# Two attention blocks in fp32: the second layer's value product is divided in halves twice, its score sums and factor sums get fixed places, and the last two sub-product groups of each twice divided convolution are interleaved in a new order

## The chip, the cores and the metric

The kernel runs on one core of one Trainium2 chip. The metric is the time on the device of one execution, in microseconds. The kernel before takes 2795.72 us (median of three runs, 2795.53 to 2796.02). A separate execution was recorded by the profiler, and every duration below that isn't called a run's comes from that record.

The names of the engines are those of the profile: PE is the matrix engine (PEld is its loading of weights, which overlaps the matmuls), DVE the vector engine, ACT the scalar engine, POOL the general engine, SP the engine whose queue issues nearly all DMA transfers.

## The reference, cut to what matters

Eight images x of 512 channels and 32 x 32 = 1024 tokens go through two layers, all in fp32. Layer 0 is attention with eight heads, layer 1 attention with one:

```python
def layer0(x):                                  # x: (8, 512, 1024)
    h = group_norm(x, 32 groups)
    q, k, v = (w_qkv @ h + b_qkv) per head      # 8 heads of 64 channels
    weight = softmax(q^T k / 8)                 # per head, 1024 x 1024
    a = v weight^T
    return x + w_proj @ a + b_proj

def layer1(x):
    xn = group_norm(x, 8 groups)
    q, k, v = q_w @ xn + q_b, k_w @ xn + k_b, v_w @ xn + v_b
    attn = softmax(q^T k / sqrt(512))           # one head, 1024 x 1024
    out = attn v
    return x + p_w @ out + p_b
```

The kernel uses two products of weights in layer 1. With m made of q's and k's weights, the scores are (m h)^T h, so g = m h takes the place of q and k. With z made of v's and p's weights, the value product and the output projection are one product: z = (p_w v_w) h, and the output is x + z attn^T + bias. "Layer 1's value product" in this text is this z, 512 channels by 1024 tokens for each image.

## The kernel before, in words

**Strassen-Winograd, once and twice.** A product of two matrices is divided into quarters and made with seven products of half the size in place of eight, at the price of sums of the quarters before and after. `wino` (L229) does this once: `step(p)` runs product p, PE accumulates several products in the same PSUM bank ("a", "b" or "c", two tiles each), and ACT or DVE takes the bank out, adding what other products left (`upper`, `done`). `conv2` (L517) does it twice for a 1 x 1 convolution: each of the seven outer products is again divided, so there are 49 products. It works on the outer products in four groups, called pairs here because most hold two: `pair(0, (1, 5))`, `pair(1, (2, 6))`, `pair(2, (7,))`, `pair(3, (3, 4))`. Each pair goes to `inner_steps` (L441), which runs the seven inner products, every one for both outer products of its pair.

**The order inside a pair** is written out by hand. `inner_steps` runs product 1, which opens bank a; ACT copies the bank into bank b (L472), on which products 6, 7 and 4 then accumulate. Next comes `finish()`, which runs what the previous pair left behind, and then 6, 2, 5, 7. Products 3 and 4 are put on a list, `tail`, and so run behind product 1 of the next pair. Product 5 opens bank c, from which DVE or ACT takes `c5` before product 3 accumulates on the same bank:

```python
            step(1)
            finish()
            for g in early:
                g()
            for j in (6, 5, 2, 7) if five_first else (6, 2, 5, 7):
                step(j)
            for g in after7:
                g()
            tail.extend([lambda: step(3), lambda: step(4)])
```

The last pair of a convolution has its copy in two halves (`halved`, L471), and in the projection p its order is 6, 5, 2, 7 (`five_first`). After every step one function of the list `background` runs (`run_background(1)`), which is how sums on DVE and POOL are spread over a stage; `hooks` are functions that run after product 7 of a pair, `after7`.

**Which convolutions are divided how.** v, k, q and p of layer 0 and g (weights m) of layer 1 run in `conv2`. z runs in `by_token` (L368), once divided: 56 matmuls of 128x128 weights on 256 columns per image, with h as the stationary operand. v runs in `conv2` with `by_tokens=True`: h is stationary too, and each matmul is 128 columns wide. The product of scores with values (`values1`, L801) and the scores of layer 1 (`scores1`, L721) are divided once and twice.

**Weights.** The sums of the weights are made once, in `prologue` (L905) and during the first attention (the dictionary `later`), and stored in DRAM. `prepare` (L281) makes the first level of sums, `keep` (L296) stores it for weights that are divided once, and `keep2` (L302) makes the second level with four POOL operations and stores it in seven transfers. `load_weight` (L329) brings a weight back into a pool of three buffers in the order of the list `uses`; a twice divided weight comes in two parts.

**What an image passes through.** In the main loop (L1141) one period holds layer 0's attention of image b, then layer 1 of image b-1 and the convolutions of image b+1: attention0, g (`layer1_scores`, L1106), scores1, z, values1 (`layer1_rest`, L1117), v (`values`), k and q (`keys_and_queries`), p (`projection2`), and the attention again. The sums of h (`image_factors`, L352, the first level; `inner_factors`, L412, the second) are made ahead, those of the next image during z and values1 (`factors_ahead`, L996). One special case at the end: the last image but one has g, scores1, z and values1 behind a once divided p, and the last image has them at the very end. So z runs eight times, v in `conv2` seven times, k, q and p seven times, g eight times.

**Around z.** `scores1` ends with seven divided products whose results ACT turns into exponentials, eight tiles e[c, cc, r] of 128 x 2 x 512 (r the half of keys, c the half of queries). `add_up` (L752) sums them on POOL into two tiles `parts` and from there into `total`; two ones-matmuls' worth of column sums (`reciprocals`, L604) then give r, the reciprocals, which DVE computes from a copy that went through DRAM and came back, and which come back a last time as rows. `right_sums` (L163) makes the factor sums of e that values1 needs: eight steps t1, t2, b12, t4, each for two halves. Here four of them run on DVE and four on POOL (`engines`, L793), all from the background list. `left_sums` (L149) makes eight sums of z. In values1 `done` (L822) multiplies each output by r, adds the bias and x, and stores it.

**What sets the order on the engines.** Every matmul is wrapped in `tc.keep_in_program_order`, so PE runs them as written. On the other engines an instruction that is wrapped keeps the written order ("pinned" in this text); the others are placed by the framework's own planning. SP's queue is in the order in which transfers were issued.

Of the kernel before, what the change touches and what calls it, by code (L numbers as in the profile page):

```python
# [9 lines left out]
F32 = mybir.dt.float32  # L10
# [19 lines left out]
def two_attention_blocks_kernel(  # L30
# [143 lines left out]
    def main_path(ctx):  # L174
# [125 lines left out]
        wdram2 = {n: dram.tile([P, 7, 7, P], F32, name=f"sums2_{n}") for n in "qkmvp"}  # L300

        def keep2(n, t, engine=nc.gpsimd):  # L302

            if engine is nc.gpsimd:
                u = wpool.tile([P, 4, 7, P], F32, tag="w", name=f"prepare2_{n}")
                u = [u[:, i, :, :] for i in range(4)]
            else:
                u = [big_tile(f"prepare2_{n}_{i}", (P, 7, P)) for i in range(4)]
            quarter = lambda k, i: t[:, :, k, ts(i, P)]
            a11, a21, a12, a22 = quarter(0, 0), quarter(0, 1), quarter(1, 0), quarter(1, 1)  # L310
            s1, s2, s3, s4 = u
            for dst, x, y, op in (
                (s1, a21, a22, ALU.add), (s2, s1, a11, ALU.subtract), (s3, a11, a21, ALU.subtract),
                (s4, a12, s2, ALU.subtract),
            ):
                tc.keep_in_program_order(engine.tensor_tensor(dst, x, y, op))
            for j, f in enumerate((a11, a12, s4, a22, s1, s2, s3)):
                nc.sync.dma_start(wdram2[n][:, :, j, :], f)
# [4 lines left out]
        for b in range(1, B - 1):  # L323
            uses += [*twice["m"], "z", *layer0, *twice["p"]]
        uses += ["p", *twice["m"], "z"]
        uses += [*twice["m"], "z"]
# [114 lines left out]
        def inner_steps(uid, parity, k, mm, add, y, x, extra, after7, final, early=(), defer=None, flush=None, five_first=False, halved=False):  # L441
# [23 lines left out]
            def step(j):  # L465
                if j == 1:
                    bank("a")
                    mm(ps["a"], 1, True)

                    bank("b")  # L470
                    for part in [slice(i, i + 1) for i in range(k)] if halved else [slice(0, k)]:  # L471
                        nc.scalar.copy(ps["b"][:, part, :], ps["a"][:, part, :])  # L472
                elif j == 6:
                    mm(ps["b"], 6, False)
                    put([keep_tmp("u2", "u")], "b", (0, 1))
                    while flush:
                        flush.pop(0)()
                    extra(0, 1, True, False)
                elif j == 2:
                    mm(ps["a"], 2, False)  # L480
                    put(y(0, 0), "a", (0, 0))
                    extra(0, 0, True, True)
                elif j == 5:
                    bank("c")
                    mm(ps["c"], 5, True)
                    put([keep_tmp("c5", "w")], "c", (1, 1))
                    extra(1, 1, True, False)
                elif j == 7:
                    mm(ps["b"], 7, False)
                    add(y(1, 1), ps["b"], [tmp["c5"]])  # L490
                    extra(1, 1, False, True)
                elif j == 3:
                    mm(ps["c"], 3, False)
                    add(y(0, 1), ps["c"], [tmp["u2"]])
                    extra(0, 1, False, True)
                elif j == 4:
                    mm(ps["b"], 4, False)
                    if defer is None:
                        put(y(1, 0), "b", (1, 0))
                    else:  # L500
                        add(y(1, 0), ps["b"], x(1, 0), (0,))
                        defer.append(lambda: add(y(1, 0), ps["b"], x(1, 0), (1,)))
                    extra(1, 0, True, True)
                run_background(1)

            step(1)
            finish()
            for g in early:
                g()
            for j in (6, 5, 2, 7) if five_first else (6, 2, 5, 7):  # L510
                step(j)
            for g in after7:
                g()
            tail.extend([lambda: step(3), lambda: step(4)])
            tail.extend(final)

        def conv2(n, f, bias, name, hooks=(), after=(), by_tokens=False, alone=False):  # L517
# [43 lines left out]
            def pair(s, products, y, x, final):  # L561
# [20 lines left out]
                def extra(r, cc, read, done):  # L582
# [6 lines left out]
                inner_steps(  # L589
                    f"{name}_{s}", s % 2, len(products), mm, add, written, x and (lambda *at: blocks(x, *at)),  # L590
                    extra, hooks.pop(0) if hooks else (), final, (), second if s == 1 else None, second if s == 2 else None, five_first=alone and s == 3, halved=s == 3,
# [4 lines left out]
            pair(0, (1, 5), [(1, 0), (1, 1)], None, [])  # L596
            pair(1, (2, 6), [(0, 0), (0, 1)], [(1, 0), (1, 0)], [load_weight, lambda: biased_half(0, 0)])
            weights2.append(weight_part((n, 1)))
            pair(2, (7,), [(1, 0)], [(0, 1)], [lambda: biased_half(1, 1)])
            pair(3, (3, 4), [(0, 1), (1, 0)], [(0, 1), (1, 0)], [load_weight, *after])  # L600
# [120 lines left out]
        def scores1(f, gf, gsteps, first, uid, stats):  # L721
# [8 lines left out]
            parts = [pair_tile(f"sum{r}_{uid}") for r in range(2)]  # L730
# [21 lines left out]
            def add_up(r, c):  # L752

                on = lambda dst, x, y: lambda: tc.keep_in_program_order(nc.gpsimd.tensor_tensor(dst, x, y, ALU.add))  # L754
                if r == c:
                    return [on(parts[r], e[c, 0, r], e[c, 1, r])]
                return [
                    *(on(parts[r], parts[r], e[c, cc, r]) for cc in range(2)),
                    on(total[:, r, :], parts[r][:, 0, :], parts[r][:, 1, :]),
                ]  # L760

            def product(s, p, y, x, before, small, after7=(), final=()):
# [13 lines left out]
                inner_steps(  # L776
                    f"{uid}_{s}", s % 2, 2, mm, add, lambda *at: blocks(y, *at), x and (lambda *at: blocks(x, *at)),
                    extra, after7, final, [lambda: background.extend(small), *(lambda q=q: factors(q) for q in before)],
                )

# [7 lines left out]
                6, 4, (1, 0), (1, 0), [], stats[10:] + add_up(1, 1) + add_up(0, 1), (),  # L788
                [lambda: exps(1, 0), lambda: background.extend(add_up(1, 0) + steps)],
            )  # L790

            t = [[pair_tile(f"t{n}_{uid}_{cc}") for cc in range(2)] for n in (1, 2, 4)]
            engines = [nc.vector] * 4 + [nc.gpsimd] * 4  # L793
            fs, steps = right_sums(
                [(e[0, cc, 0], e[0, cc, 1]) for cc in range(2)], [(e[1, cc, 0], e[1, cc, 1]) for cc in range(2)],
                [lambda cc, n=n: t[n][cc] for n in range(3)],
                lambda *a: engines.pop(0).tensor_tensor(*a, ALU.subtract),
            )
            return total, {p: [x[:, i, :] for x in fs[p] for i in range(2)] for p in fs}

        def values1(b, zf, ef, r, xt, uid, hooks):  # L801
            last = b == B - 1

            def mm(p, i, ps, start):
                cut = 2 if last and (p, i) == (3, 1) else 1
                for part in range(cut):
                    cols = ts(part, HT // cut)
                    for k in range(4):
                        matmul(
                            ps[:, cols], zf[p][k // 2][:, k % 2, ts(i, P)], ef[p][k][:, cols],  # L810
                            start=start and k == 0, stop=k == 3, skip_group_check=True,
                        )

            def added(xh, o, oc):
                nc.vector.scalar_tensor_tensor(xh, o, obias[1][:, oc : oc + 1], xh, ALU.add, ALU.add)  # L815
# [6 lines left out]
            def done(i, row, c, ps, u):  # L822
# [15 lines left out]
                nc.vector.tensor_mul(o, o, r[:, c, :])  # L838
                added(xh, o, oc)
# [65 lines left out]
        def prologue():  # L905
# [46 lines left out]
            for f in p0_steps:  # L952
# [7 lines left out]
            load = lambda: load_weight(tc.keep_in_program_order)  # L960
            later = {
                3: steps, 4: [lambda: tc.keep_in_program_order(keep("z", t)), load], 8: [load], 12: [
                    load,
# [31 lines left out]

        def factors_ahead(h, loads, applies, uid):  # L996
# [3 lines left out]
            def begin():  # L1000
                for f in loads:
                    f()
                hf, t = image_factors(h, uid)
# [3 lines left out]
                hooks[3] += [*applies[2:], inner[1], *t[2:4]]  # L1007
                hooks[4] += [*inner[2:4], lambda: background.extend([*t[4:6], *inner[4:6], *t[6:], inner[6]])]
# [108 lines left out]
        def layer1_rest(b, inner, gf, gsteps, stats, hooks, ahead):  # L1117
            first = query_factors(gf[1], f"1_1_{b}")
            total, ef = scores1(inner, gf, gsteps, first, f"1_{b}", stats)
            state = {}  # L1120

            def sums():
                state["r"] = reciprocals([total], f"1_{b}", True, nc.sync)

            z = by_token(
                weight("z"), hf, f"z1_{b}", hooks=[*hooks, [sums]], back=3,
                after=[load_weight, lambda: background.extend(zsteps)],
# [3 lines left out]
            stiles = [big_tile(f"sz{i}_{b}", (P, 2, 2, C // 2)) for i in (1, 2, 4)]  # L1131
            halves = lambda t: (t[:, :, : C // 2], t[:, :, C // 2 :])
            zf, zsteps = left_sums(
                [halves(t) for t in z[:2]], [halves(t) for t in z[2:]],
                [lambda j, t=t: t[:, j, :, :] for t in stiles], nc.vector.tensor_add, nc.vector.tensor_sub,
# [3 lines left out]
        here = lambda *t: tc.keep_in_program_order(nc.vector.tensor_sub(*t))  # L1139
        x1, plan = None, {}  # L1140
        for b in range(B):  # L1141
# [31 lines left out]
            if last:  # L1173
# [12 lines left out]
                layer1_rest(b - 1, inner, gf, gsteps, stats, [[], mean, [], affine], ahead)  # L1186
# [250 lines left out]
```

## Time and profile before

| what | us |
|---|---|
| median of three runs | 2795.72 |
| profiled execution, whole | 2796.04 |
| its span, first to last instruction | 2794.2 |
| one period, attention of image 2 to attention of image 3 (first score matmuls at 664.56 and 1005.96) | 341.4 |
| in it: attention0, to the start of g at 780.35 | 115.8 |
| g, to the start of scores1 at 801.34 | 21.0 |
| scores1, to the start of z at 843.93 | 42.6 |
| z, to the start of values1 at 863.58 (two of its seven products run behind values1's first, until 877.46) | 19.7 |
| values1, to the start of v at 904.93 | 41.4 |
| v, to the start of k at 938.99 (values1's last products run between) | 34.1 |
| k, to the start of q at 960.89 | 21.9 |
| q, to the start of p at 982.28 | 21.4 |
| p, to the attention at 1005.89 | 23.6 |

How to read it: the stages overlap at their borders, since the last products of a stage run behind the first one of the next. The times are starts of matmuls. An instruction in the profile is named by its output and inputs, with buffer numbers left out, then by the number of partitions and elements; "x4" behind it is a count. In this program one fp32 matmul is shown as two passes, and a start in the trace is the time from which a pass's place in the stream can be read. An engine's busy time counts what it executes; waits for other engines' results show as idle time before an instruction, in square brackets with the name of what ended the wait.

### The profile page before, as it was taken

The page shows a single profiled execution, that of the slowest core. Times are in us where ns is not written, and L with a number is a line of the kernel's source. Part 1 is how long each engine was busy: PE and PEld are TensorE (multiplying, and loading weights), DVE is VectorE, ACT ScalarE, POOL GpSimd, SP SyncE. Part 2 cuts the span into 40 slices and gives each one's busy share as a digit, 9 for nine tenths or more (in the row PEclk, how much of TensorE's full clock was granted, in tenths as well). Part 3 has the DMA queues.
Part 4 walks back from the last instruction along what each step waited for, and adds up shares of the span by engine and source line. Part 5 has one row for each costly group of instructions (what it writes and reads, how often), then busy time and mean ns, then how long its engine had stood idle before and what let it go on. Part 6 is the DMA issues. An engine that isn't in the chain of part 4 may idle for free.

```text
span 2794.2 us, 35149 instructions
## 1 busy us (share of the span) xinstructions
PE 2781.3 (100%) x12764; PEld 1753.0 (63%) x12764; DVE 1991.5 (71%) x3022; ACT 990.9 (35%) x1311; POOL 1269.1 (45%) x1300
## 2 busy tenths in 40 slices
PE   9999999999999999999999999999999999999999
PEld 6437637676376853858538584485844868348585
DVE  6577777677777677766786767776677766787665
ACT  1253463214531246312553125531254213633130
POOL 2303605745077430865308652185612846037672
PEclk9999999999999999999999999999999999999999
DMA  7835412344113441134401443114522045112301
GB/s 263 254 132 184 179 32 70 129 156 153 39 62 134 158 154 32 62 143 161 149 24 62 162 183 108 32 54 162 203 88 63 23 152 218 54 62 88 122 3 73
DMA packets 118669, 320.10 MB, mean 115 GB/s; under 512 B 19607, under 2 KB 58199, under 8 KB 107866
## 3 DMA queue, kind: packets, MB, share of 16 engines
q1 hardware_dynamic: 117902, 317.36, 32.0%
q8 instruction: 103, 1.69, 0.2%
q14 instruction: 76, 0.62, 0.1%
q10 hardware_dynamic: 588, 0.42, 0.0%
HBM read 247.13 MB, written 70.62 MB: 114 GB/s over the span
## 4 chain that ended last, share of the span: by engine, by line
PE 99%; DVE 1%; issue 0%; DMA 0%; SPq 0%
PE sc L60 16%; PE av L60 16%; PE psb_av L60 6%; PE psb L60 5%; PE psa_av L60 4%; PE psc_av L60 4%; PE psc L60 3%; PE psa L60 3%; PE psb_z L60 3%; PE psb_v L60 3%; PE psb_g L60 3%; PE psb_q L60 3%; PE psb_k L60 3%; PE psb_p L60 3%; PE psa_z L60 2%; PE psc_z L60 2%
## 5 line engine op out<-in xcount | busy, mean ns | idle before, releaser
L669 ACT ACTIVATE e<-sc 128x1024 f32<-128x1024 f32 x512 | 476.1, 1050 | 72.9 <-PE sc L60 72.9
L673 DVE TENSOR_TENSOR sum<-sum,e 128x1024 f32<-128x1024 f32 x384 | 470.6, 1225 | 35.7 <-ACT e L669 1.1
L60 PE MATMUL sc<-q,k 64*128 64x512 f32 x2048 | 456.8, 596 | 0.0
L60 PE MATMUL av<-e,v 128*64 128x512 f32 x2048 | 453.4, 595 | 0.0
L60 PEld LDWEIGHTS sc<-q,k 64*128 64x128 f32 x2048 | 190.0, 185 | 246.1 <-ACT e L669 121.5
L60 PEld LDWEIGHTS av<-e,v 128*64 128x64 f32 x2048 | 141.4, 137 | 299.0 <-issue 288.2
L423 POOL TENSOR_TENSOR inner_h<-x 128x256 f32<-128x256 f32 x16 | 14.8, 923 | 416.2 <-DVE x L1139 416.2
L671 DVE TENSOR_TENSOR sum<-e,e 128x1024 f32<-128x1024 f32 x64 | 79.1, 1236 | 106.8 <-ACT e L669 106.8
L692 ACT COPY a<-av 128x512 f32<-128x512 f32 x64 | 37.5, 587 | 320.0 <-PE av L60 280.5
L126 POOL TENSOR_TENSOR rstd<-ve,mhalf 128x4 f32<-128x4 f32 x16 | 19.4, 1210 | 265.8 <-DVE ve L124 265.8
L60 PE MATMUL psb<-inner,inner_h 128*128 128x256 f32 x448 | 115.6, 380 | 0.0
L60 PE MATMUL psa_av<-e,z 128*128 128x512 f32 x256 | 113.3, 595 | 0.0
L423 POOL TENSOR_TENSOR inner_h<-h 128x256 f32<-128x256 f32 x30 | 25.2, 841 | 180.3 <-DVE h L1139 112.6
L754 POOL TENSOR_TENSOR sum<-sum,e 128x1024 f32<-128x1024 f32 x32 | 81.3, 2541 | 28.7 <-ACT e L750 27.4
L60 PEld LDWEIGHTS psb<-inner,inner_h 128*128 128x128 f32 x448 | 84.5, 190 | 13.6 <-POOL inner L438 2.1
L472 ACT COPY psb_v<-psa_v 128x256 f32<-128x256 f32 (+1 forms) x35 | 15.5, 442 | 217.8 <-DVE x L815 155.4
L60 PE MATMUL psb_g<-inner_h,w_m 128*128 128x256 f32 x336 | 86.8, 383 | 0.2
L740 DVE TENSOR_TENSOR e<-psc,u 128x512 f32<-128x512 f32 x56 | 38.7, 691 | 66.2 <-PE psc L60 66.2
L552 POOL TENSOR_TENSOR v<-v,v 128x256 f32<-128x256 f32 x28 | 20.3, 727 | 144.1 <-DVE u_v L547 143.9
L60 PEld LDWEIGHTS psa_av<-e,z 128*128 128x128 f32 x256 | 48.0, 190 | 57.3 <-issue 56.6
L750 ACT ACTIVATE e<-e 128x1024 f32<-128x1024 f32 x64 | 65.1, 1052 | 46.1 <-DVE e L740 25.2
L745 POOL TENSOR_TENSOR e<-e,e 128x512 f32<-128x512 f32 x64 | 79.4, 1273 | 2.3 <-DVE e L740 2.2
(437 smaller groups left out, 6102.9 us busy)
## 6 DMA issues: line engine op xcount, KB each, us to landing
r<-all_rows SPq DMA_DIRECT2D x78, 256.0 KB
x<-in_x SPq DMA_DIRECT2D x36, 512.0 KB
h<-in_x SPq DMA_DIRECT2D x32, 512.0 KB
spill<-x SPq DMA_DIRECT2D x32, 512.0 KB
x<-spill SPq DMA_DIRECT2D x32, 512.0 KB
out<-x SPq DMA_DIRECT2D x63, 256.0 KB
kept<-a SPq DMA_DIRECT2D x28, 512.0 KB
again<-kept SPq DMA_DIRECT2D x28, 512.0 KB
```

What stands on the lines that cost most here:

```text
L60: tc.keep_in_program_order(nc.tensor.matmul(*args, **kw))
L126: nc.gpsimd.tensor_tensor(rstd, ve, mhalf, ALU.pow)
L423: pin(engine.tensor_tensor(dst, x, y, ALU.subtract))
L552: nc.gpsimd.tensor_tensor(d, x, y, ALU.add)
L669: nc.scalar.activation(e, sc, AF.Exp, scale=(C // 8) ** -0.5)
L671: nc.vector.tensor_add(total, es[0], e)
L673: nc.vector.tensor_add(total, total, e)
L692: nc.scalar.copy(dst, av)
L740: nc.vector.tensor_add(dst[0], ps, x[0])
L745: nc.gpsimd.tensor_tensor(blocks(dst, r, cc)[0], blocks(x, r, cc)[0], blocks(y, r, cc)[0], ALU.add)
L750: nc.scalar.activation(e[c, cc, r], e[c, cc, r], AF.Exp, scale=scale)
L754: on = lambda dst, x, y: lambda: tc.keep_in_program_order(nc.gpsimd.tensor_tensor(dst, x, y, ALU.add))
```

## The change

There are two parts, and smaller edits that go with the first.

**z in halves twice.** z runs in `conv2` with `by_tokens=True` on `inner`, the twice divided sums of h that g and scores1 use already. Its weights get the second level of sums: `keep2` is cut into steps (`keep2_steps`), and the first attention's dictionary `later` runs the four POOL operations at its places 5, 7, 9 and 11 and the seven stores at place 12, where `keep("z", t)` was at 4. `uses` loads z's weights in two parts. z now comes out by channel tiles with tokens along the free axis, so `stiles`, `halves` and the index in values1 change shape.

**Sums around z.** `add_up` no longer uses `parts`: it adds halves straight into `total`, on POOL for r == c and on DVE for r != c. The eight factor sums of e are all on POOL and pinned, in the order b12, t2, t1, t4, two behind pair 1 of z and six behind pair 3. The column sums (`sums`) are issued behind pair 2 of z, where they were at its end. z's left sums are pinned on DVE, the first four run directly behind the convolution and the rest from the background list. In values1 the multiply by r and the add behind it are pinned for the first two outputs, and the first-level sums of the next image in `factors_ahead` are pinned too, six of them in one hook. In the case of the last image but one, the two statistics hooks of the norm move from pairs 1 and 3 of z to pairs 0 and 1.

**The last two pairs interleaved.** `inner_steps` no longer runs its steps but returns `step` and `run`. `conv2` sets up pair 3 first, and gives its product 1 to pair 2 to run between 2 and 5. In pair 3 the two products that pair 2 left (3 and 4) get a place by hand:

| | before | after |
|---|---|---|
| v, k, q, g (z after) | pair 2: 1, (3, 4 of pair 1), 6, 2, 5, 7; pair 3: 1, (3, 4 of pair 2), 6, 2, 5, 7 | pair 2: 1, (3, 4 of pair 1), 6, 2, **1 of pair 3**, 5, 7; pair 3: (3), 6, (4), 2, 5, 7 |
| p | the same, pair 3 ends 6, 5, 2, 7 | pair 3: (3), 6, 5, (4), 7, 2 |

The copy of bank a into bank b is one instruction in every pair.

The diff, cut to its core:

```diff
-        wdram2 = {n: dram.tile([P, 7, 7, P], F32, name=f"sums2_{n}") for n in "qkmvp"}
-
-        def keep2(n, t, engine=nc.gpsimd):
+        wdram2 = {n: dram.tile([P, 7, 7, P], F32, name=f"sums2_{n}") for n in "qkmvpz"}
+
+        def keep2_steps(n, t, engine=nc.gpsimd, pin=lambda ins: ins):
...
+            def store():
+                for j, f in enumerate((a11, a12, s4, a22, s1, s2, s3)):
+                    pin(nc.sync.dma_start(wdram2[n][:, :, j, :], f))
...
+        def keep2(n, t, engine=nc.gpsimd):
+            for f in keep2_steps(n, t, engine):
+                f()
...
-            uses += [*twice["m"], "z", *layer0, *twice["p"]]
-        uses += ["p", *twice["m"], "z"]
-        uses += [*twice["m"], "z"]
+            uses += [*twice["m"], *twice["z"], *layer0, *twice["p"]]
+        uses += ["p", *twice["m"], *twice["z"]]
+        uses += [*twice["m"], *twice["z"]]
...
-                    for part in [slice(i, i + 1) for i in range(k)] if halved else [slice(0, k)]:
-                        nc.scalar.copy(ps["b"][:, part, :], ps["a"][:, part, :])
+                    nc.scalar.copy(ps["b"], ps["a"])
...
-            step(1)
-            finish()
...
-            for j in (6, 5, 2, 7) if five_first else (6, 2, 5, 7):
-                step(j)
...
+            def run():
+                if order is None:
+                    step(1)
+                    finish()
+                    steps = [6, 2, *between, 5, 7]
+                else:
+                    three, four, *rest = tail
+                    tail.clear()
+                    steps = [{-3: three, -4: four}.get(j, j) for j in order] + rest
...
+                for j in steps:
+                    j() if callable(j) else step(j)
...
+            return step, run
...
-            pair(2, (7,), [(1, 0)], [(0, 1)], [lambda: biased_half(1, 1)])
-            pair(3, (3, 4), [(0, 1), (1, 0)], [(0, 1), (1, 0)], [load_weight, *after])
+            ahead, end = pair(
+                3, (3, 4), [(0, 1), (1, 0)], [(0, 1), (1, 0)], [load_weight, *after],
+                order=(-3, 6, 5, -4, 7, 2) if alone else (-3, 6, -4, 2, 5, 7),
+            )
+            pair(
+                2, (7,), [(1, 0)], [(0, 1)], [lambda: biased_half(1, 1)], flush=second, between=[lambda: ahead(1)],
+            )[1]()
+            end()
...
-            parts = [pair_tile(f"sum{r}_{uid}") for r in range(2)]
...
-                on = lambda dst, x, y: lambda: tc.keep_in_program_order(nc.gpsimd.tensor_tensor(dst, x, y, ALU.add))
+                engine = nc.gpsimd if r == c else nc.vector
+                on = lambda *a: lambda: tc.keep_in_program_order(engine.tensor_tensor(*a, ALU.add))
+                dst, terms = total[:, r, :], [e[c, cc, r][:, i, :] for cc in range(2) for i in range(2)]
                 if r == c:
-                    return [on(parts[r], e[c, 0, r], e[c, 1, r])]
...
+                    return [on(dst, *terms[:2]), *(on(dst, dst, t) for t in terms[2:])]
+                return [on(dst, dst, t) for t in terms]
...
-                6, 4, (1, 0), (1, 0), [], stats[10:] + add_up(1, 1) + add_up(0, 1), (),
-                [lambda: exps(1, 0), lambda: background.extend(add_up(1, 0) + steps)],
+                6, 4, (1, 0), (1, 0), [], stats[10:] + add_up(1, 1), (),
+                [lambda: exps(1, 0), lambda: background.extend(add_up(0, 1) + add_up(1, 0))],
...
-            engines = [nc.vector] * 4 + [nc.gpsimd] * 4
...
+            on = lambda *a: lambda: tc.keep_in_program_order(nc.gpsimd.tensor_tensor(*a))
+            steps = [
+                on(dst[cc], x[cc], y[cc], op) for dst, x, y, op in (
+                    (b12, b22, b12, ALU.subtract), (t2, b12, b11, ALU.add), (t1, b22, t2, ALU.subtract),
+                    (t4, b21, t2, ALU.subtract),
+                ) for cc in (1, 0)
+            ]
...
-                            ps[:, cols], zf[p][k // 2][:, k % 2, ts(i, P)], ef[p][k][:, cols],
+                            ps[:, cols], zf[p][i][:, ts(k, P)], ef[p][k][:, cols],
...
-                nc.vector.tensor_mul(o, o, r[:, c, :])
-                added(xh, o, oc)
+                pin = tc.keep_in_program_order if (row, c) == (0, 0) else lambda ins: ins
+                pin(nc.vector.tensor_mul(o, o, r[:, c, :]))
+                added(xh, o, oc, pin)
...
+            second = keep2_steps("z", t, pin=tc.keep_in_program_order)
             later = {
-                3: steps, 4: [lambda: tc.keep_in_program_order(keep("z", t)), load], 8: [load], 12: [
-                    load,
+                3: steps, 4: [load], 5: second[:1], 7: second[1:2], 9: second[2:3], 11: second[3:4], 12: [
+                    second[4], load, load,
...
-                hf, t = image_factors(h, uid)
+                hf, t = image_factors(h, uid, here)
...
-                hooks[3] += [*applies[2:], inner[1], *t[2:4]]
-                hooks[4] += [*inner[2:4], lambda: background.extend([*t[4:6], *inner[4:6], *t[6:], inner[6]])]
+                hooks[3] += [*applies[2:], inner[1], *t[2:]]
+                hooks[4] += [*inner[2:4], lambda: background.extend(inner[4:])]
...
-            z = by_token(
-                weight("z"), hf, f"z1_{b}", hooks=[*hooks, [sums]], back=3,
-                after=[load_weight, lambda: background.extend(zsteps)],
-            )
+            z = conv2(
+                "z", inner, None, f"z1_{b}", [hooks[0], [*hooks[1], *esteps[:2]], [*hooks[2], sums], [*hooks[3], *esteps[2:]]],
+                after=[lambda: [f() for f in zsteps[:4]], lambda: background.extend(zsteps[4:])], by_tokens=True,
+            )
...
-                layer1_rest(b - 1, inner, gf, gsteps, stats, [[], mean, [], affine], ahead)
+                layer1_rest(b - 1, inner, gf, gsteps, stats, [mean, affine, [], []], ahead)
```

## The prediction

> **What bounds the kernel now.** I read the page's head and its chain first, then the matmul groups by form, then the timeline at the stages that the change touches, and last the chain of waits for what PE stands still for.
>
> ```profile
> span 2794.2 us, 35149 instructions
> PE 2781.3 (100%) x12764; PEld 1753.0 (63%) x12764; DVE 1991.5 (71%) x3022; ACT 990.9 (35%) x1311; POOL 1269.1 (45%) x1300
> ...
> PE 99%; DVE 1%; issue 0%; DMA 0%; SPq 0%
> ```
>
> PE is the bound from end to end, at a granted clock of 1.0. The chain of waits charges it with 4.9 us in all, at four places in the first 250 us. So a microsecond counts only if PE gets fewer or narrower matmuls, or if a short stall among them goes. Stalls under 150 ns hide in "busy"; I read them from starts.
>
> One fp32 matmul stands in the trace as two passes (z: 56 matmuls per image, 896 passes in 8 images). What a pass costs is the distance of starts, not its own duration:
>
> ```profile
> 849.11 3.62 PE L60 MATMUL psb_z<-w_z,t_h 128*128 128x256 f32 x16
> 852.56 3.62 PE L60 MATMUL psa_z<-w_z,x 128*128 128x256 f32 x16
> ...
> 919.55 1.05 PE L60 MATMUL psb_v<-w_v,inner_h 128*128 128x128 f32 x8
> 920.44 0.61 PE L60 MATMUL psa_v<-w_v,h 128*128 128x128 f32 x4
> ```
>
> Columns: start, length, engine. 256 wide: 3.45/16 = 216 ns a pass. 128 wide, in v, which is already halved twice by tokens: 0.89/8 = 112 ns.
>
> The second thing to see is the stall inside each twice divided convolution. Here it is in k, and a second one in p:
>
> ```profile
> 955.90 0.59 PE L60 MATMUL psa_k<-t_h,w_k 128*128 128x256 f32 x2
> 956.33 0.59 PE L60 MATMUL psc_k<-h,w_k 128*128 128x256 f32 x2
> 956.53 0.75 ACT L472 COPY psb_k<-psa_k 128x256 f32<-128x256 f32 x2 [4.13 <-PE psa_k L60]
> 956.76 1.70 PE L60 MATMUL psb_k<-inner_h,w_k 128*128 128x256 f32 x6
> 957.33 0.73 PEld L60 LDWEIGHTS psb_k<-inner_h,w_k 128*128 128x128 f32 x4 [0.38 <-ACT psb_k L472]
> 958.30 0.38 PE L60 MATMUL psa_k<-h,w_k 128*128 128x256 f32 x1
> ...
> 1004.13 0.59 PE L60 MATMUL psc_p<-t_a,w_p 128*128 128x256 f32 x2
> 1004.83 1.13 PE L60 MATMUL psb_p<-inner_a,w_p 128*128 128x256 f32 x4
> ```
>
> The last pair's product 1 (psa_k) is copied by ACT into bank b, and product 6 waits for the copy: six passes from 956.76 to 958.30 take 1.54 us where 6 x 0.216 = 1.30, so 0.24 us is lost. In p product 4 waits for the add behind product 7: 0.70 where 0.43 is due, and the next four passes take 1.06 to 1005.89 where 0.86 is due, of which I count 0.10 to the restart: 0.37 us.
>
> **The change part by part.**
>
> *z in halves twice.* Removed per image: 7 products x 16 passes x 216 ns = 24.2 us. Added: 7 x 7 products x 2 matmuls x 2 passes = 196 passes (v has 1372 in 7 images, the same 196) x 112 ns = 21.95 us. Gain 2.23 us, all on PE, x 8 images = **17.8 us**.
>
> A rule of the Trainium skill speaks against this (TensorE: Matmul & The Clock Gate, "Back-to-back issue gap"): in a stream of weight loads and matmuls the narrow matmul doesn't cost its share of columns; 128 wide sustains some 81 ns where the isolated formula gives 56. The row that bears on it:
>
> ```profile
> 919.60:942.00 22.40, 22.40 (x195) 22.12 (x194) 15.38 (x35) 4.56 (x9) 5.69 (x8) 1.00 0.30 106
> ```
>
> (window, its length, busy PE, PEld, DVE, ACT, POOL.) In the v stage the weight loads are busy 22.12 of 22.40 us, so they are near binding. With the page's factor 81/56 on half of 216 ns, a pass would cost 156 ns and z 30.6 us, an estimate: 6.4 us worse per image, 51 us in all. But the starts in this very stage stand 112 ns apart, 2x2 passes of the same form and operands as z gets. I take the row. Break-even is 24.2/196 = 123 ns.
>
> *The last pair's product 1 ahead.* Old order: (last pair but one) 5, 7; (last pair) 1; (but one) 3, 4; (last) 6. New: 1, 5, 7, 3, 6, 4. Between 1 and 6 there are now 5, 7, 3 = 1.30 us in place of 0.86; the copy needs 0.42 (last pass start to ACT start: 956.12 to 956.53) + 0.57 (a 512 wide copy, undivided now) + 0.05: covered. Removed per image: v 0.23, k 0.24, q 0.24, p 0.26 + 0.37, g 0.26 = 1.60 us (each read as above); 7 images and an eighth g: 11.5 us.
>
> But 5 writes bank c, DVE must add it out (c_k, 0.42 us) before 3 accumulates on the same bank, and what covered that was product 1. Now only 7 stands between. From 5's last pass start: 0.42 to DVE's start + 0.42 + 0.05 = 0.88 us; PE has that pass and 7: 0.216 + 0.432 = 0.65. New wait 0.24, and 0.10 to restart: 0.34 us for q, p, g. For v the result is 0.10 us sooner and 7 is 0.45 long: 0.30. In k the variance matmul of the next norm (0.14) stands between: 0.20. In z the column sums (863.01 to 863.58: 0.57) do: none. Sum 0.30 + 0.20 + 3 x 0.34 = 1.52 per image, x 7 + 0.34 = 11.0 us. So the stall goes from ACT's copy to DVE's: **0.5 us gained**, p's second stall being most of what pays for it (2 now stands between 7 and its 3, 4). Bounds: 11.5 gained if the wait isn't there, 3 lost if it is 0.1 longer each.
>
> *Work that PE doesn't see.* Per image DVE loses four t-steps and ten z and w_z adds, and gets 30 adds of z out of PSUM (four of 0.69 at 512 wide, the others 0.42) and 8 half adds of the score sums; POOL takes all 8 t-steps (2.35 each) and z's sums (eight of 0.73), and gives half of the score sums away. Four places where PE could wait:
>
> - First pair of z, product 7 waits for ACT's copy of 6, which is queued behind two exps:
>
> ```profile
> 848.24 1.03 PE L60 MATMUL psb<-g,inner_h 128*128 128x256 f32 x4
> 849.24 2.00 ACT L750 ACTIVATE e<-e 128x1024 f32<-128x1024 f32 x2 [1.07 <-DVE e L740]
> ```
>
>   The score product ends at 849.11, its exps at 851.24, the copy 0.59 later, at PE 851.88. PE has 6, 2, 5 = 2.69 until 851.80. Wait 0.08 + 0.07 restart = 0.15 us: **1.2 us** in 8 images. Between 0 and 0.3 each.
> - Second pair, 3 waits for c on DVE, behind the 8 pinned adds. These are spread one a step; DVE's starts in a row stand 0.61 (512) and 0.33 (256) apart. Counted through from the first exp, c is out 12.8 us into z and PE is there at 13.1. I take 0. If adds and pieces cost their full 0.68 and 0.42 (nothing overlapped), c is 0.93 us late.
> - values1's third product (5) needs t1 from POOL. POOL can begin when DVE's sums are done, some 11.5 us into z, and needs 2 x 2.35 + 8 x 0.73 + 4 x 2.35 = 20 us; PE is there after 22.6 + 6.9 + 1.8 + 6.9 = 38 us. Slack 6 us. POOL against DVE with both operands in SBUF is slower: 2.35 turns into 3.33 (the t-step groups of POOL), still inside.
>
> ```profile
> 853.44 1.32 DVE L797 TENSOR_TENSOR t<-e,e 128x1024 f32<-128x1024 f32 x1
> 853.44 4.61 DVE L797 TENSOR_TENSOR t<-e,e 128x1024 f32<-128x1024 f32 x2
> ```
>
>   The first line is the step alone, 1.32; the second has it with the next, which runs beside a POOL step and takes 3.29. The new DVE adds fall where POOL is idle, the moved t-steps where DVE reads PSUM mostly.
>
> - In values1 the first outputs' multiply by r is pinned now. Behind it on DVE stand four sz sums, two of the next image's t_h and u_av, which product 7 needs 29 us into values1; with 6 us for these, r and the first two x must be in by 23. Before, r was issued 5.3 us into values1 and x up to 8.3. Cost 0.
>
> *Loads and first image.* SP's queue per image: z's load becomes two (3.2 MB for 1.8), the second ahead of v's, and v's second part moves behind z's second pair; the row sums go out some 6 us earlier, so r, x and the next h land earlier (all_rows left at 867.2 against values1's start at 863.6). Nothing there is late. The last norm's two small matmuls only change places (0.14 each). In image 0 seven stores of z (3.2 MB) stand ahead of v's second and k's first load, after the r transfers at 214. Seven such stores took SP 117.6 to 124.4; with 15 us for them v's load lands by 240. v needs it at 234 + 13 = 247. Cost 0; without that cover at most a few us, once.
>
> *Sum.* On the profiled execution (2796.0 us with its launch, span 2794.2): -17.8 - 0.5 + 1.2 = -17.1. It stands 0.3 us over the median of the runs, 2795.7. Forecast **2778.6 us**.
>
> **The rivals.**
> - *The order pays in full.* Were c read in time, all 11.5 us of stalls go: 2767.6. For it: the 1.30 us of cover for the copy. Against: bank c's read takes 0.88 us by three rows, its cover 0.65. Chance 0.13.
> - *DVE is late in z.* The 0.93 us of the second pair, + 0.07 restart, in 8 images: +8, 2786.6. For it: only 0.3 us of margin after eight more DVE instructions. Against: back-to-back DVE starts overlap. Chance 0.15.
> - *The narrow passes don't get narrow enough* (near 123 ns): z pays nothing, 2796. For it PEld's 22.12 of 22.40; against it 112 ns in v. Chance 0.06: no change.
> - *Slower: t1 is late on POOL.* At values1's product 5. It decides when PE waits there by more than 17.1/8 = 2.1 us per image, that is POOL 8 us behind my count. If all 6 + 8 of its operations ran at 3.33/2.35 of their time, 20 us become 28.5 and the wait is 2.4: 2798; beyond 0.2% at a wait of 2.9 us, some 2802. Chance 0.04.
>
> **How the numbers follow.** My forecast has 0.62, its own range 2774 to 2783 (0 to 0.3 us for the ACT wait, 0.1 each way on the new wait). About 0.2% (5.6 us) is what a measurement can tell from none. Faster: 0.62 + 0.13 + 0.15 = 0.90; same 0.06; slower 0.04. Leaving out the last two and the tails, 2766 to 2787.5.
>
> **What the changed profile would show.** z's passes 112 ns apart, 98 matmuls per image, values1 starting 1.9 to 2.3 us sooner after z's start; the period from one attention to the next 339.3 us (1005.96 - 664.56 = 341.4 before). After product 5 and 7 of each last pair but one PE waits 0.2 to 0.35 us for DVE's c, and no more for ACT's copy; p's 4 follows 3 at once. In z PE waits at most 0.2 us, for ACT. I am wrong if c's read doesn't hold PE (then lower), if z's second pair stands still for DVE, or values1's third product for POOL.

## The result: 2781.4 us

The changed kernel takes **2781.39 us** (median of five runs, 2780.78 to 2781.74) against 2795.89 us for the kernel before beside it (2795.53 to 2796.02): 14.5 us less, a ratio of 0.9948 with a 95% interval of 0.9934 to 0.9963. The forecast was 2778.6 us, its likeliest case 2774 to 2783. The profiled execution took 2781.39 us, 14.65 us less than the profiled one before.

The head of the page and its chain, after:

```profile
span 2779.6 us, 36877 instructions
PE 2764.8 (99%) x13436; PEld 1761.6 (63%) x13436; DVE 2052.0 (74%) x3214; ACT 1000.3 (36%) x1307; POOL 1297.5 (47%) x1384
...
PE 97%; DVE 2%; DMA 0%; issue 0%; ACT 0%; SPq 0%; DVEq 0%
```

PE is still the bound, with 672 more passes (a matmul is two) and 16.5 us less busy time. Now 2% of the chain lies on DVE, where 1% did: places where PE waits for DVE. To find them, I took the distance from each matmul pass to the next one, less the usual distance of its form (112 ns at 128 columns, 216 at 256, 429 at 512), and summed what is left by stage. I call it the stall of a stage. Both traces read in this way give what follows; the forecast by stages is the new wait less the old one of the prediction, times 7 images (8 for g), as 7 x (0.30 - 0.23) for v.

| part | forecast, us | measured, us |
|---|---|---|
| z's passes (193.5 before, 175.6 after) | -17.8 | -17.9 |
| stalls in z and at the head of values1 | +1.2 | +1.7 |
| stalls in v | +0.5 | +1.7 |
| in k | -0.3 | +0.5 |
| in q | +0.7 | +0.8 |
| in p | -2.0 | -2.0 |
| in g | +0.6 | +0.8 |
| start-up, scores, column sums, the end | 0 | -0.3 |
| sum | -17.1 | -14.7 |

**z's passes are right to 0.1 us.** From z's start to values1's, by windows (window, its length, busy PE, PEld, DVE, ACT, POOL, granted clock, DMA):

```profile
842.69:865.49 22.80, 22.80 (x197) 22.00 (x196) 18.51 (x37) 6.10 (x10) 11.16 (x11) 1.00 0.18 62
```

The timeline of the changed kernel in z's first two pairs (columns: start, length, engine; the times in brackets are idle time before an instruction and what ended it):

```profile
845.31 1.05 PE L60 MATMUL psb_z<-w_z,inner_h 128*128 128x128 f32 x8
845.44 2.00 ACT L776 ACTIVATE e<-e 128x1024 f32<-128x1024 f32 x2 [1.09 <-DVE e L766]
846.20 0.61 PE L60 MATMUL psa_z<-w_z,x 128*128 128x128 f32 x4
...
847.35 0.56 ACT L472 COPY u_z<-psb_z 128x512 f32<-128x512 f32 x1
847.99 1.14 PE L60 MATMUL psb_z<-w_z,inner_h 128*128 128x128 f32 x8
```

Eight passes take 0.89 us from 845.31 to 846.20, 112 ns each, as in v. The copy of product 6 runs behind the two exps, ends at 847.91, and product 7 restarts inside the eight passes from 847.99, which is 0.08 us of wait (0.15 was forecast).

```profile
854.90 0.74 DVE L566 TENSOR_TENSOR c_z<-psc_z,z 128x256 f32<-128x256 f32 x2
855.22 0.61 PE L60 MATMUL psa_z<-w_z,x 128*128 128x128 f32 x4
855.69 0.71 PE L60 MATMUL psc_z<-w_z,x 128*128 128x128 f32 x4
```

In the second pair DVE ends c at 855.64, 12.95 us into z. Product 3 was due on PE at 855.66 and starts at 855.69: 0.03 us late, and then 0.10 us to restart, in nearly every image. The margin of 0.3 us that I had counted there wasn't left.

**The stall went from ACT's copy to DVE's c,** as forecast. The timeline of q in the changed kernel, to be held against k before:

```profile
973.73 0.59 PE L60 MATMUL psc_q<-inner_h,w_q 128*128 128x256 f32 x2
974.16 0.59 PE L60 MATMUL psb_q<-inner_h,w_q 128*128 128x256 f32 x2
974.37 0.42 DVE L566 TENSOR_TENSOR c_q<-psc_q,q 128x256 f32<-128x256 f32 x1 [0.64 <-PE psc_q L60]
974.84 0.30 PEld L60 LDWEIGHTS psc_q<-h,w_q 128*128 128x128 f32 x2 [0.49 <-DVE c_q L566]
974.84 0.70 PE L60 MATMUL psc_q<-h,w_q 128*128 128x256 f32 x2
975.38 0.59 PE L60 MATMUL psb_q<-inner_h,w_q 128*128 128x256 f32 x2
```

Product 5 (bank c) starts at 973.73, product 7 at 974.16, and product 3, on bank c again, at 974.84 where 974.59 was due: 0.25 us. Its two passes then take 0.54 in place of 0.43: 0.10 us. 0.35 us in q, p and g (0.34 forecast), 0.33 in v (0.30). z has the column sums in that place; what it loses behind them, 0.40 us, is what the kernel before loses behind its column sums too.

**k is where the count was short.** In each image it has a second wait, at product 4:

```profile
953.01 1.24 DVE L168 TENSOR_TENSOR t_a<-again 128x512 f32<-128x512 f32 x1
953.15 0.70 PE L60 MATMUL psc_k<-h,w_k 128*128 128x256 f32 x2
953.68 1.65 PE L60 MATMUL psb_k<-inner_h,w_k 128*128 128x256 f32 x6
954.17 0.41 DVE L566 TENSOR_TENSOR k<-psb_k,c_k 128x256 f32<-128x256 f32 x1
```

The add of product 7 (k<-psb_k,c_k) sits on DVE behind a factor sum of the next projection, t_a, which takes 1.24 us. Product 4 needs the bank from which that add reads, and loses 0.19 us, 0.09 of wait and 0.10 of restart. With 0.22 us at product 3, k has 0.41 us where 0.20 was forecast.

v has two waits that come once: at the first v 0.3 us more than before (what holds it there was not followed up), and 0.73 us at 1257.4, where v's first product on bank c waits for values1's last outputs, which DVE had left behind statistics of the next image.

### The profile page after: what moved, and what is told of

Its sections match the earlier page's. It is cut to its first block, busy times and chain, and to the rows that moved or that the text cites. A ratio compares the mean times of both kernels' runs of the same rounds, so it can differ in the third digit from the quotient of the medians.

```text
span 2779.6 us, 36877 instructions
## 1 busy us (share of the span) xinstructions
PE 2764.8 (99%) x13436; PEld 1761.6 (63%) x13436; DVE 2052.0 (74%) x3214; ACT 1000.3 (36%) x1307; POOL 1297.5 (47%) x1384
## 4 chain that ended last, share of the span: by engine, by line
PE 97%; DVE 2%; DMA 0%; issue 0%; ACT 0%; SPq 0%; DVEq 0%
PE sc L60 16%; PE av L60 16%; PE psb_av L60 5%; PE psb L60 5%; PE psa_av L60 4%; PE psc_av L60 4%; PE psc L60 4%; PE psa L60 3%; PE psb_k L60 3%; PE psb_z L60 3%; PE psb_q L60 3%; PE psb_p L60 3%; PE psb_g L60 3%; PE psb_v L60 3%; PE psc_v L60 2%; PE psc_p L60 2%
## 5 line engine op out<-in xcount | busy, mean ns | idle before, releaser
L482 ACT COPY psb_v<-psa_v 128x512 f32<-128x512 f32 (+1 forms) x28 | 14.5, 517 | 234.0 <-DVE x L845 178.1
L60 PE MATMUL psb_z<-w_z,inner_h 128*128 128x128 f32 x672 | 87.5, 276 | 0.1
L60 PEld LDWEIGHTS psb_z<-w_z,inner_h 128*128 128x128 f32 x672 | 81.4, 192 | 0.8 <-ACT u_z L472 0.3
L482 ACT COPY psb<-psa 128x512 f32<-128x512 f32 x56 | 31.9, 570 | 130.2 <-PE psa L60 130.2
```

The costliest lines, as they stand in the source:

```text
L60: tc.keep_in_program_order(nc.tensor.matmul(*args, **kw))
L482: nc.scalar.copy(ps["b"], ps["a"])
```

## Experiments

### The order undone

```diff
-                if order is None:
-                    step(1)
-                    finish()
-                    steps = [6, 2, *between, 5, 7]
...
+                step(1)
+                finish()
+                steps = order or [6, 2, 5, 7]
...
+            pair(2, (7,), [(1, 0)], [(0, 1)], [lambda: biased_half(1, 1)], flush=second)[1]()
+            pair(
+                3, (3, 4), [(0, 1), (1, 0)], [(0, 1), (1, 0)], [load_weight, *after],
+                order=(6, 5, 2, 7) if alone else (6, 2, 5, 7), halved=True,
+            )[1]()
```

> The changed kernel with the old order of the last two pairs and the halved copy: only z, the sums and the loads differ from the kernel before. Theory (the stall only moved from ACT's copy to DVE's read of bank c): 11.5 us of old stalls come back and the new ones go, which the changed kernel's trace puts at 12.9 us (q, p, g 0.35 per image, v 0.33, k 0.41), so 1 to 2 us faster than the changed kernel, 2779.5 to 2780.5. Rival (the new order pays 11.5 us): 2793.

Measured: 2782.07 us (2781.51 to 2783.24), 0.7 us slower than the changed kernel by the medians, not faster; the runs of the two overlap by 0.2 us. By stages v, k, q and g are 2.9 us better with the old order, p 1.9 worse, as the theory has it. But z is 1.8 us worse: as a twice divided convolution it has the copy's stall too, 0.2 us in each image, which the expectation forgot. So in this kernel the new order just about pays for itself, through z.

### The order alone

The kernel before, with `inner_steps` and `conv2` of the changed kernel.

> The kernel before with only the new order and the undivided copy. Theory: same as the kernel before within 2 us, 2796 to 2798, with 0.35 us of wait at the last pair but one's product 3 in q, p and g. Rival (the order pays in full): 2784.5.

Measured: 2797.20 us (2796.73 to 2797.70), ratio 1.0005 (0.9997 to 1.0014). The trace shows g +0.75, k +0.5, q +0.8, v +1.0 and p -1.95 us. The rival that the order pays in full falls, and the step "0.5 us gained" is wrong by 1.6 us (by the trace) to 2.0 us (by the runs).

### Where product 1 of the last pair stands

Two variants of the changed kernel, each with one line different. In the first, product 1 stands one step later:

```diff
-                    steps = [6, 2, *between, 5, 7]
+                    steps = [6, 2, 5, *between, 7]
```

> The changed kernel with the last pair's product 1 behind product 5 in place of ahead of it: 6, 2, 5, 1 of the last pair, 7, 3. Theory: product 1 and 7 (0.86 + 0.43 us) cover DVE's read of bank c, so the 12.9 us of waits at product 3 go; ACT's copy has 7 and 3 as cover, 0.86 us for the 0.83 it needs beyond product 1's last pass, so at most 0.05 us appears at product 6. 2768.5 to 2770.5. Rival (the wait goes back to ACT's copy or to DVE's next add): 2778 to 2782.

Measured: 2773.03 us (2772.45 to 2773.68), above what was expected. The waits at product 3 are gone, but the copy is not quite covered: product 6 waits 0.05 us and takes 0.08 to restart in p and g, and 0.06 us is lost in q and 0.09 in v. A margin of 0.03 us on a sum of four readings was none. v also has three waits that come once: 0.5 us at 254.7 and at 577.0, and 0.9 us at 1254.2. The next variant has only the first of them, 0.6 us there.

In the second, product 5 comes first:

```diff
-                    steps = [6, 2, *between, 5, 7]
+                    steps = [6, 5, *between, 7, 2] if between else [6, 2, 5, 7]
```

> The changed kernel with the last pair but one as 6, 5, 1 of the last pair, 7, 2, and then 3, 6, 4 as before: every read of a bank has at least 0.86 us of other products behind it, the copy has 7, 2 and 3 (1.3 us), and 4 has 2, 3 and 6 behind 7. Theory: no wait is left at 3, 6 or 4: 2768 to 2769.5, and below the variant with product 1 one step later. Rival (DVE, with five adds in a row, is late somewhere else): 2775 to 2782.

Measured: **2768.19 us** (2767.86 to 2770.71), ratio 0.9904 (0.9888 to 0.9919), 13.2 us better than the changed kernel. The timeline of q in this variant:

```profile
968.05 0.59 PE L60 MATMUL psc_q<-inner_h,w_q 128*128 128x256 f32 x2
968.48 0.59 PE L60 MATMUL psa_q<-h,w_q 128*128 128x256 f32 x2
968.91 0.59 PE L60 MATMUL psa_q<-t_h,w_q 128*128 128x256 f32 x2
968.92 0.41 DVE L566 TENSOR_TENSOR c_q<-psc_q,q 128x256 f32<-128x256 f32 x1
969.35 0.59 PE L60 MATMUL psb_q<-inner_h,w_q 128*128 128x256 f32 x2
969.54 0.57 ACT L482 COPY psb_q<-psa_q 128x512 f32<-128x512 f32 x1 [0.41 <-PE psa_q L60]
969.78 0.59 PE L60 MATMUL psa_q<-h,w_q 128*128 128x256 f32 x2
970.21 0.59 PE L60 MATMUL psc_q<-h,w_q 128*128 128x256 f32 x2
970.64 1.46 PE L60 MATMUL psb_q<-inner_h,w_q 128*128 128x256 f32 x6
```

The starts stand 0.43 us apart throughout. c is out at 969.33, 0.88 us ahead of product 3 at 970.21; the copy is out at 970.11, half a microsecond ahead of product 6 at 970.64. The stalls fall by 2.8 us in g and v and by 2.5 in k, p and q. In both variants nothing is changed but what stands between the products, and with more between 5 and 3 the wait at product 3 is gone: it was for bank c. (k's wait at product 4 was for bank b's read behind product 7, which also has more behind it now.)

### The five-first order in the kernel before

> The kernel before with only the five-first order (z once divided as before): 6, 5, 1 of the last pair, 7, 2, then 3, 6, 4. Theory: the stalls of the old order are 11.5 us in the trace of before and none of them moves elsewhere, so 2795.7 - 11.5 = 2784.2; z in halves twice is then worth the rest to the five-first kernel's 2768.2, 16 us (17.9 on PE less its own waits). Rival (the 13.2 us between the two orders of the changed kernel come mostly from z's stage): 2790 or more.

Measured: 2785.13 us (2784.64 to 2785.41), ratio 0.9962 (0.9948 to 0.9975): 10.4 us of the 11.5 that I had counted as old stalls. Against it the five-first variant above, which differs in z and the sums, is 16.9 us faster. So z in halves twice is worth 17 us together with the sums that were moved for it (no run has the one without the other), and the order, arranged in this way, 10 us besides.

### Five first in the second pair too

```diff
-                    steps = [6, 5, *between, 7, 2] if between else [6, 2, 5, 7]
+                    steps = [6, 5, *between, 7, 2] if between else [6, 5, 2, 7] if defer is not None else [6, 2, 5, 7]
```

Only the second pair of a convolution has `defer`.

> The five-first kernel with product 5 ahead of 2 also in the second pair of each twice divided convolution (6, 5, 2, 7). Theory: z's second pair waits there 0.03 us for DVE's c and 0.10 to restart; with product 2 more between, 0.13 x 8 = 1.0 us goes: 2767.2. Rival (DVE's queue is the limit, so the order on PE doesn't help): 2768.2 and the restart of 0.10 stays.

Measured: **2766.79 us** (2766.44 to 2768.06), ratio 0.9898 (0.9881 to 0.9914), 1.4 us better by the medians than the five-first variant; the runs of the two overlap by 0.2 us. The trace shows the forecast effect: z's stalls fall by 1.06 us, and the restart in the second pair is gone. This version beats both kernels.

### How much room DVE has in z

```diff
-                return [on(dst, dst, t) for t in terms]
+                return [on(dst, dst, t) for t in terms] + [on(spare[:, r, :], t, t) for t in terms[:2]]
```

This is extra work into a tile that nothing reads.

> The changed kernel with four more half adds per image on DVE (of e to a spare tile), in the list with the eight score sums of z's first two pairs. Theory: DVE has no margin there (c of the second pair was out 12.95 us into z, PE was there at 12.92), and one more add lies ahead of c, so PE waits 0.6 to 0.75 us per image for it, 5 to 6 us: 2786 to 2788. Rival (gaps between DVE's instructions take it up): 2781.4 to 2782.5.

Measured: 2823.24 us, ratio 1.0101 (1.0084 to 1.0118), 42 us over the changed kernel where 5 to 6 were expected. The trace has z 41.8 us longer. In seven of the eight images PE waits 0.51 us for c of the second pair (as expected), then 0.20 and 0.48 us for other banks, and 2.55 us behind the column sums, where the next c is late. Only the first of these had been counted. The waits behind the column sums come to 20 of the 42 us in the eight images, and some 12 us are of another kind, in the last two lines here (by windows, columns as above):

```profile
858.50:860.60 2.10, 1.71 (x13) 1.33 (x12) 2.10 (x5) 0.36 (x1) 0.72 (x1) 1.00 0.00 0
860.60:863.40 2.80, 2.80 (x27) 2.80 (x27) 2.80 (x3) 0.00 (x0) 2.11 (x2) 1.00 0.36 71
863.40:864.60 1.20, 0.89 (x8) 0.70 (x6) 0.64 (x2) 0.00 (x0) 1.20 (x1) 1.00 0.87 349
864.60:867.90 3.30, 1.12 (x11) 0.52 (x11) 2.49 (x5) 0.57 (x1) 1.94 (x3) 0.92 0.56 235
867.90:870.80 2.90, 2.90 (x15) 2.90 (x15) 2.25 (x4) 0.00 (x0) 2.74 (x5) 0.50 0.01 3
```

After the long wait the granted clock is 0.50 for some 3 us, and 128 wide passes stand 0.213 us apart where 0.112 is usual. So DVE's lateness, the rival that I had priced at 1.0 us per image and 8 us in all, costs far more once it grows.

### How much room POOL has before values1

```diff
                     (b12, b22, b12, ALU.subtract), (t2, b12, b11, ALU.add),
+                    (t2, b12, b11, ALU.add), (t2, b12, b11, ALU.add),
```

t2 is made again with the same values. Each entry is two steps, so this is the variant with four more; with one entry there are two more, and for three more one half is put in beside it.

> The changed kernel with two more POOL steps per image in the factor sums of e (t2 made twice over). Theory (slack of 6.0 us before values1's product 5, and 2.35 to 2.8 us a step): 4.7 to 5.6 us fit, 2781 to 2782. Rival (the slack is smaller in most images): 2785 or more.

> The same with three more. 7.05 us, or 8.0 with two of the steps at 2.8, less 6.0: PE waits 1.05 to 2.0 us per image at product 5. With four more steps it waited 4.6 us and then ran at half the granted clock for some 5 us, 3.2 us more per image. Theory (a short wait doesn't bring the clock down): 8 x 1.05 to 2.0, 2790 to 2797. Rival (any wait of over 1 us brings it down): 2816 to 2823.

> The changed kernel with four more POOL steps per image in the factor sums of e: t2 is made three times over. The changed kernel's trace has t1 ready at 875.0 and values1's product 5 at 881.0, a slack of 6.0 us. Theory: 4 x 2.35 = 9.4 us of more work make PE wait 3.4 us per image, 27 us in all: about 2808; more if the longer POOL stretch meets DVE's two-operand steps (3.3 us each). Rival (POOL never holds PE, t1 has far more room): 2781 to 2783.

Measured: 2790.43, 2815.19 and 2840.72 us, ratios 0.9982 (0.9974 to 0.9989), 1.0073 (1.0057 to 1.0090) and 1.0163 (1.0146 to 1.0180). All three are above what was expected. The slack itself is as forecast: t1 was ready 6.0 us ahead of product 5 in seven images of the changed kernel, and 0.94 us ahead with two more steps. The eighth is the last image but one: 3.7 us, and with two more steps PE waits there, 1.9 us at product 5 and 2.1 us more, for DVE, at product 7. (Most of the rest of that variant's 9 us is DVE's too: 0.5 us at product 4 in five images, and v's first bank c; and 1.7 us are half a clock behind the wait of 2.1 us.) With three more the waits are 2.0 to 2.5 us in seven images and 4.7 in that one; with four more, 4.6 and over. Four more steps at one place of the trace, by windows again, and the timeline there:

```profile
885.00:887.60 2.60, 2.60 (x7) 1.14 (x6) 2.60 (x2) 2.53 (x3) 2.60 (x2) 1.00 1.09 455
887.60:892.70 5.10, 0.64 (x3) 0.03 (x1) 5.10 (x3) 0.82 (x1) 5.10 (x3) 0.93 0.43 180
...
893.70:898.50 4.80, 4.80 (x7) 2.02 (x6) 4.73 (x6) 0.00 (x0) 4.80 (x3) 0.50 0.28 109
```

```profile
887.08 10.60 POOL L820 TENSOR_TENSOR t<-e,t 128x1024 f32<-128x1024 f32 x4
887.59 5.58 DVE L1172 TENSOR_TENSOR sz<-sz,z 128x512 f32<-128x512 f32 x2
...
892.67 3.78 PE L60 MATMUL psc_av<-t,sz 128*128 128x512 f32 x4 [4.46 <-POOL t L820]
```

The wait is 4.6 us where 3.4 were due, because three of POOL's steps run beside DVE's sums of z (both with operands in SBUF) and take 2.8 us, not 2.35; DVE's two halves take 2.8 us each where an undisturbed half add takes 0.68. And after the wait PE runs at half the clock for some 6 us here.

With three more steps the wait is the same in most images, but what follows isn't:

```profile
882.90:885.84 2.94, 0.56 (x2) 0.00 (x1) 2.94 (x2) 0.86 (x1) 2.94 (x3) 1.00 0.71 302
885.84:892.00 6.16, 6.16 (x15) 2.81 (x16) 6.09 (x7) 0.00 (x0) 6.16 (x3) 1.00 0.23 88
...
2254.25:2257.22 2.97, 0.60 (x2) 0.00 (x0) 2.97 (x2) 0.86 (x1) 2.97 (x3) 1.00 0.72 304
2257.22:2260.60 3.38, 3.38 (x5) 1.41 (x6) 3.31 (x6) 0.00 (x0) 3.38 (x2) 0.55 0.18 69
```

Both waits are 2.54 us. After the first the clock stays at 1.00, after the second it is 0.55 over the next 3.4 us. The 2815 us lie next to the rival's 2816, but not by the rival's rule: in the profiled run, three of the eight waits were followed by the lower clock.

## Why the prediction was right, and where it was off

- **z's passes.** Right to 0.1 us: -17.9 against -17.8, and 17 us by the two five-first kernels. The rule of the Trainium skill that, taken as a factor, would have made it 51 us slower (TensorE: Matmul & The Clock Gate, "Back-to-back issue gap") does not carry over to this fp32 form: the weight loads are busy 22.00 of the 22.80 us from z's start to values1's, and the passes still stand 112 ns apart. The row decides. One sign was put wrongly: values1's start does not come 1.9 to 2.3 us sooner after z's start, but 3.2 us later (22.80 against 19.65), since less of z is left to run behind values1's first product (1.8 us against 6.9). It is values1's second product that comes sooner, by 2.1 us (31.46 against 33.53).
- **The order.** The mechanism was right, the stall goes from ACT's copy to DVE's read of bank c, and the size of one such stall too (0.35 for 0.34). The sum "0.5 us gained" was wrong down to its sign: by stages it is 1.8 us lost, still within the bounds that I gave (3 lost). That the total stayed in its range rests on z's passes. Of the 2.3 us between the two, 0.8 is k, where I had followed bank c and not the next read in DVE's queue, product 7's, behind a factor sum of another stage; 1.2 is v, 1.0 of it in the two waits that come once. Without z the order costs 1.5 us; had z kept the old order, its copy would have cost 1.8, a credit that stood in no line of my sum.
- **z's waits.** 1.7 for 1.2 us. ACT's was half as large (0.08 for 0.15); DVE's was 0.13 where I had taken 0. I had counted DVE's starts 0.61 us apart, but score sums that follow each other on the same half of the total stand some 0.72 apart (846.19, 846.90 and 847.63), where two on different halves start 0.60 apart (849.84 and 850.44), and so the margin was gone.
- **POOL's slack.** 6.0 us as forecast, but 3.7 in the last image but one, which I had not looked at apart from the others.
- **The slower rival was under-priced.** I had it decide at 2.1 us of wait per image and come to 2802 at 2.9. Three more steps made PE wait 2.0 to 2.5 us in seven images and 4.7 in one, 20 us in all by the list of waits, and gave 2815: the clock that falls behind such waits was in no step of mine.
- **Scores, loads and the first image** took what was forecast, nothing, to within 0.5 us. I took SP's time from 117.6 to 124.4 for that of seven stores; it holds five of p's seven and one other. Nothing hung on it.

## What to carry to other kernels

When an order is changed to cover one reader of a bank, list every read and write of every bank in the new order with the work that stands between, and not just the pair that was the trouble: here the better order was one line away and worth 13 us. A resource whose margin is down to 0.1 us is not hidden, it is the next bound, and an instruction put on it is paid in full or more: four half adds on DVE in z, 0.68 us each, cost 5.2 us per image. Narrow matmuls are priced by a row of the same type and width in the trace, not by a general figure.

## What the runs showed of the hardware

- **A short standstill of PE can halve its clock.** Over all variants, of PE's waits of 1.4 to 2.0 us behind long busy stretches none of four was followed by the lower clock; of those of 2.1 to 2.6 us, nine of thirteen; of those of 4.5 us and more, all ten. It cost 1.5 to 3.1 us each time, and took some 3 to 6 us to come back. The Trainium skill (TensorE: Matmul & The Clock Gate, "Part 1: The HAM clock gate (the "warmup" mystery)") describes an activity window of some 3.4 us that runs freely, and so a loss that depends on where a wait falls. The traces show such a window. Ahead of the kernel's end, each low stretch of the variants with more DVE or POOL steps lasts 3.41 us or twice that, and within each of these four traces their borders fit a grid of 3.413 us. On this grid the equal waits differ: none of the eight that were not followed by the lower clock has more than 2.10 us in one step of the grid, and of the nineteen that were, eighteen have 2.12 us or more in one step (the last has 2.04, with 0.48 us of an earlier wait in the same step). So a wait of 2.5 us is or isn't followed by the lower clock according to how a border of the grid divides it, and 2.1 us in one step were enough here, less than the 3.4 us that the page names.
- **A restart costs PE 0.07 to 0.10 us.** Behind a wait, even one of 0.03 us, the first pass takes this much more than its place: 0.10 at 855.69 in z and at 974.84 in q of the changed kernel, 0.07 at product 6 where product 1 stands one step later.
- **POOL and DVE slow each other down when both read SBUF.** With four more steps, POOL's step of 1024 columns goes from 2.35 to 2.80 us, DVE's half add from 0.68 to up to 2.8. A DVE add of which one operand is in PSUM keeps its 0.42 us beside a POOL step (880.49 in the same trace).
